# Layer 3's gathered rows as three bfloat16 parts, and fifteen instead of seventeen dense tiles

## The chip, the cores and the metric

The kernel runs on one core of a Trainium2 chip, in one launch. The metric is the device time of that core in microseconds (us), as the median of several runs.

## What is computed

The program is a graph network of four layers on one set of 3750 nodes with 256 features and 60000 edges, sorted by destination. Each layer has a graph part (gnn) and a feed-forward part (ffn). The change concerns layer 3's graph part, two hypergraph convolutions:

```python
def _hconv(x, W, b, src, dst, n):
    xt = x @ W
    ones = jnp.ones(src.shape, xt.dtype)
    D = jax.ops.segment_sum(ones, src, num_segments=n)
    B = jax.ops.segment_sum(ones, dst, num_segments=n)
    Dinv = jnp.where(D > 0, 1.0 / D, 0.0)
    Binv = jnp.where(B > 0, 1.0 / B, 0.0)
    m = jax.ops.segment_sum(xt[src], dst, num_segments=n) * Binv[:, None]
    out = jax.ops.segment_sum(m[dst], src, num_segments=n) * Dinv[:, None]
    return out + b
h = _prelu(_hconv(x, W1, b1, src, dst, n), a)
h = _hconv(h, W2, b2, src, dst, n) + x
return _prelu(h, a)
```

Its input x is the layer norm of the nodes, and its result is added to them. All of it is float32. The destinations are drawn as the square of a uniform number, so low destinations have many edges and high ones few.

## The kernel before, in words

**Tiles.** The nodes are 30 tiles (NT) of 128 (P). Each convolution has three parts: the product with W (`conv_in`, L2245), the sums over edges to the destinations (`to_dst`, L2207), and the sums back to the sources (`to_src`, L2226). Both sums go through `sums` (L2163), in one of two ways.

**Dense.** For the first TD = 17 tiles of destinations there are count matrices: for destination tile t and source tile S a block of 128 x 128 holds the number of edges between each pair of nodes. Tile 0 has so many edges that it has two of them, so there are NV = 18 slabs of 30 blocks. Summing over a block is a matmul. Blocks are bfloat16 (small whole numbers, exact), and the float32 rows are split into three bfloat16 parts whose sum is the row (`split`, L2155: copy, subtract, copy, subtract, on ACT and DVE in turn). So a block costs two matmuls: 512 columns (two parts) into `two_ps` (L2184), and 257 columns (third part and a column of ones that counts the edges) into `third_ps` (L2186).

**Gathered.** The last 13 tiles of destinations have few edges. `CAPS` (L41) gives for every tile the number of chunks of 128 edges: 12 to 10 a tile, 3 for the last, 131 for those 13. For a chunk, POOL issues one indirect DMA (`gather`, L150) that fetches 128 float32 rows of 1 KB from a table in DRAM. DVE compares the place of each edge in its tile with a row of 0 to 127, which makes a one-hot matrix (L2173), and one float32 matmul with 257 columns (L2186) adds the chunk into `third_ps`. Chunks are taken in groups of G = 5 that share a buffer `gt` (five buffers) and a one-hot buffer `oh` (two buffers). ACT puts a column of ones into each `gt` (L2170). Nothing else of these tiles uses `two_ps`.

**To the destinations.** A dense tile loads its slab (`adT`, 960 KB, on SP's queue, four buffers), sums, divides by the count, and is split into `two["m"]`, `third["m"]`, which stay in SBUF. A gathered tile gathers from `xtab`, the table of x @ W, sums, and writes its rows to the table `mtab`. The order is written out: two dense tiles, then thirteen times a gathered and a dense one, then two dense ones.

**To the sources.** For each of the 30 source tiles the same blocks in the other orientation (`ad`, loaded for two source tiles at a time) give 18 dense products with the rows of `m`. The edges to destinations outside the dense tiles are gathered from `mtab`, JS = 5 chunks a source tile. `finish` then makes the tile's result: `between` adds the bias, applies prelu and does the next layer's `conv_in`; `last` (L2259) adds x, updates the nodes and begins the ffn (`enter`).

**conv_in** transposes a tile on PE, multiplies by W, copies the product to SBUF, writes it to `xtab` on SP's queue, and splits it into `two["x"]`, `third["x"]`. The order of instructions on each engine comes from a scheduler that follows the program's priorities; it puts most of the blocks of the first dense tile between the products of the first `conv_in`.

**The blocks** are built during and behind layer 2's ffn by `dense_blocks` (L2068). While edges are read, `put` (L355 to L423) gives each edge a place in a table `blocks` of NCB = 840 columns: NV + SPLIT = 23 columns for each source tile are for dense tiles (the first five slabs have two), JS = 5 for gathered ones. `dense_blocks` reads the first 690 columns, makes one-hots from them (L2112), multiplies pairs of one-hots on PE into one PSUM buffer (L2098), casts on ACT (L2099), transposes them again on PE and writes `adT` and `ad`. There are 36 halves of 15 tiles; some are asked for by layer 2's sums (`beside_l2_sums`, L2064, six at each of its calls), and what is left comes behind the ffn. The other 150 columns are read at the start of `l3_gnn` (L2142), which makes the indices of the gathers from `mtab` from them.

Of the kernel before, what the change touches and what calls it, by code (L numbers as in the profile page):

```python
# [10 lines left out]
F32 = mybir.dt.float32  # L11
# [10 lines left out]
P = 128  # L22
# [11 lines left out]
TD = 17  # L34
NV = TD + 1
SPLIT = 5
JS = 5
# [1779 lines left out]
class Regular(Gnn):  # L1817
# [250 lines left out]
    def dense_blocks(self, pool, wp, op, pp):  # L2068
# [7 lines left out]
        got = pool.tile([P, K], I32, name="db_got")  # L2076
        nc.sync.dma_start(got, self.blocks.rearrange("(p k) a -> p (k a)", p=P)[:, :K])
# [46 lines left out]
    def l3_gnn(self, entry):  # L2124
# [3 lines left out]
        G = 5  # L2128
        with ExitStack() as outer:
            keep, sp, gp, wp, xp, pp, tp, ep = self.pools(outer, l3=1, l3s=4, l3g=5, l3w=2, l3x=2, l3p=-2, l3tp=-1,  # L2130
                                                          l3ep=-2)
# [4 lines left out]

            idx = dict(x=self.srci[:, SP0:], m=keep.tile([P, JS * NT], I32, name="l3_idxm"))
            loc = dict(x=self.dloc[:, SP0:], m=keep.tile([P, JS * NT], F32, name="l3_locm"))
            with ExitStack() as st:
                pool, = self.pools(st, l3i=1)  # L2140
                got = pool.tile([P, JS * NT], I32, name="l3_got")
                nc.scalar.dma_start(got, self.blocks.rearrange("(p k) a -> p (k a)", p=P)[:, NCB - JS * NT:])  # L2142
                part = pool.tile([P, JS * NT], I32, name="l3_part")
                nc.vector.tensor_scalar(part, got, 255, None, op0=ALU.bitwise_and)
                nc.vector.tensor_copy(loc["m"], part)
                nc.vector.tensor_scalar(part, got, 8, None, op0=ALU.arith_shift_right)
                nc.vector.tensor_scalar(idx["m"], part, -float(TD * P), 0.0, op0=ALU.add, op1=ALU.max)

            two, third = {}, {}
            for n, k in (("x", NT), ("m", TD)):  # L2150
                two[n] = keep.tile([P, k, 2, D], BF16, name="l3_two" + n)
                third[n] = keep.tile([P, k, D + 2], BF16, name="l3_third" + n)
                nc.vector.memset(third[n][:, :, D:], 1.0)

            def split(n, t, v):  # L2155
                hm, lo = two[n][:, t], third[n][:, t, :D]
                nc.scalar.copy(hm[:, 0], v)
                r = wp.tile([P, D], F32, name="rest")
                nc.vector.tensor_tensor(r, v, hm[:, 0], ALU.subtract)
                nc.scalar.copy(hm[:, 1], r)  # L2160
                nc.vector.tensor_tensor(lo, r, hm[:, 1], ALU.subtract)

            def sums(n, blocks, table, cols):  # L2163


                rows = []
                for c in range(0, len(cols), G):
                    some = cols[c:c + G]
                    gt = gp.tile([P, G, D + 1], F32, name="gt")
                    nc.scalar.copy(gt[:, :, D], self.ones[:, :G])  # L2170
                    oh = wp.tile([P, G, P], F32, name="oh")
                    k = slice(some[0], some[-1] + 1, some[1] - some[0] if len(some) > 1 else 1)
                    nc.vector.tensor_tensor(oh[:, :len(some)], self.iota.unsqueeze(1).to_broadcast([P, len(some), P]),  # L2173
                                            loc[n][:, k].unsqueeze(2).to_broadcast([P, len(some), P]), ALU.is_equal)
                    for j, k in enumerate(some):
                        self.gather(gt[:, j, :D], table, idx[n][:, k:k + 1])
                        rows.append((oh[:, j, :], gt[:, j, :]))
                ps3 = pp.tile([P, D + 2], F32, name="third_ps")
                all3 = [(block, third[n][:, t, :D + 1]) for block, t in blocks] + rows
                if blocks:  # L2180
                    ps = pp.tile([P, 2, D], F32, name="two_ps")
                for i, (block, rhs) in enumerate(all3):
                    if i < len(blocks):
                        nc.tensor.matmul(flat(ps), block, flat(two[n][:, blocks[i][1]]),  # L2184
                                         start=(i == 0), stop=(i == len(blocks) - 1))
                    nc.tensor.matmul(ps3[:, :D + 1], block, rhs, start=(i == 0), stop=(i == len(all3) - 1))  # L2186
# [6 lines left out]
                if not blocks:  # L2193
                    nc.scalar.mul(o, ps3[:, :D], has)
                    return o
# [6 lines left out]
            def slab_of(v):  # L2202
                slab = sp.tile([P, NV * 2 * P], BF16, name="slab")
                nc.sync.dma_start(slab[:, :NT * P], self.adT[v])
                return slab

            def to_dst(xtab, mtab):  # L2207
                def dense(t):
                    slabs = [slab_of(v) for v in ((0, 1) if t == 0 else (t + 1,))]
                    split("m", t, sums("x", [(slab[:, S * P:(S + 1) * P], S) for slab in slabs for S in range(NT)],  # L2210
                                       None, []))

                def sparse(t):
                    c = sum(CAPS[TD:t])
                    o = sums("x", [], xtab, list(range(c, c + CAPS[t])))
                    nc.sync.dma_start(mtab[(t - TD) * P:(t - TD + 1) * P], o)
                first = TD - (NT - TD) - 2
                for t in range(first):
                    dense(t)
                for i in range(NT - TD):  # L2220
# [90 lines left out]
```

## Time and profile before

| | |
|---|---|
| runs, median (lowest to highest) | 5742.64 us (5733.62 to 5743.11) |
| profiled execution, its own time | 6525.78 us |
| its span; mean granted clock of PE | 6524.0 us; 0.798 |
| busy in it: PE, DVE, POOL, ACT | 70%, 47%, 45%, 32% of the span |
| layer 3's graph part in it | 4749 to 5986 us |
| all matmuls of L2184 and L2186, from blocks and gathers | 2046 and 3284 records |

The profile is one execution in which engines and DMA queues were recorded. Times in windows, waits and chains are us from the start of its span. A row of "waits" names the engine and line that waited, then what it waited for: us in total, times, longest. "issue" is a wait for nothing that the profile shows. In a timeline the bracket is the idle time before an instruction and what ended it. Float32 matmuls leave two records each, and a few records can be missing.

### The profile page before, as it was taken

What the parts mean: (1) busy time and instruction counts of PE and PEld (TensorE: products, weight loads), DVE (VectorE), ACT (ScalarE), POOL (GpSimd) and SP (SyncE); (2) the same over time, 40 slices, a digit from 0 to 9 for tenths busy, and PEclk for the clock granted to TensorE, in tenths of its full rate; (3) what the DMA queues carried; (4) which work ended last, traced back from release to release, by engine and by line L of the source; (5) the groups of instructions that cost most, each with busy time, mean ns of one, the idle gap of its engine ahead of it and who ended that gap; (6) DMA issues with size and microseconds to landing.
All of it is one profiled execution on the core that took longest, in us unless ns stands there. A gap on an engine that the chain in (4) does not pass through costs nothing. (4 is left out here: it accounts for less than half of the span.)

```text
span 6524.0 us, 64749 instructions
## 1 busy us (share of the span) xinstructions
PE 4544.5 (70%) x20324; PEld 3306.5 (51%) x20438; DVE 3068.4 (47%) x7333; ACT 2064.1 (32%) x4862; POOL 2921.8 (45%) x2845
## 2 busy tenths in 40 slices
PE   6826655596476665975555553798879898896885
PEld 2425554465455553634444442576545565564673
DVE  5634433794233346435565557403532342266435
ACT  1125544312455552324343442222531121110121
POOL 0046666676566658864444440012025444452124
PEclk9957777798677777987777775698589999998896
DMA  4334444202344431145555551222434554455113
GB/s 147 132 95 115 115 116 112 43 2 72 99 119 117 115 79 35 22 130 160 159 159 157 147 148 45 90 91 74 162 124 139 137 134 128 132 145 162 50 56 114
DMA packets 431195, 714.02 MB, mean 109 GB/s; under 512 B 117474, under 2 KB 308645, under 8 KB 426748
## 3 DMA queue, kind: packets, MB, share of 16 engines
q0 software_dynamic: 145168, 379.81, 23.0%
q1 hardware_dynamic: 267064, 316.47, 15.5%
q10 hardware_dynamic: 18612, 13.50, 0.7%
q8 instruction: 166, 2.72, 0.2%
q14 instruction: 185, 1.52, 0.1%
HBM read 583.81 MB, written 125.15 MB: 109 GB/s over the span
## 5 line engine op out<-in xcount | busy, mean ns | idle before, releaser
L1965 PE MATMUL sum_ps<-gt,oh 128*128 128x260 f32 (+2 forms) x3150 | 1018.8, 485 | 368.2 <-issue 155.4
L1965 PEld LDWEIGHTS sum_ps<-gt,oh 128*128 128x128 f32 x3150 | 749.4, 244 | 565.0 <-issue 187.7
L150 POOL DMA_INDIRECT gt<-l_vk,srci x525 | 497.6, 948 | 549.1 <-issue 179.4
L156 POOL DMA_INDIRECT blocks<-put x480 | 648.2, 1350 | 155.0 <-issue 145.6
L150 POOL DMA_INDIRECT gt<-l_h,srci x525 | 496.6, 946 | 333.8 <-issue 228.8
L150 POOL DMA_INDIRECT gt<-l_feat,g x525 | 501.7, 956 | 317.2 <-issue 235.2
L1947 DVE TENSOR_TENSOR gt<-gt,bank 128x1792 f32<-128x1792 f32 x225 | 453.5, 2016 | 123.6 <-remote 52.8
L1839 ACT ACTIVATE oh<-iota,dloc 128x128 f32<-128x128 f32 x1575 | 481.4, 386 | 19.1 <-PE sum_ps L1965 15.7
L150 POOL DMA_INDIRECT gt<-l_mtab,l_idxm x300 | 296.3, 988 | 359.9 <-ACT gt L2170 184.3
L150 POOL DMA_INDIRECT gt<-l_xtab,srci x262 | 253.2, 966 | 396.7 <-DMA l_xtab<-xt 192.4
L2184 PE MATMUL two_ps<-l_twox,slab 128*128 128x512 bf16 x1026 | 354.8, 391 | 28.1 <-issue 27.8
L147 PE MATMUL y_ps<-f_w,hT 128*128 128x256 f32 x1600 | 359.4, 384 | 15.5 <-DVE y L1075 13.5
L2184 PEld LDWEIGHTS <-slab 128*128 128x128 bf16 x2160 | 213.5, 99 | 268.2 <-issue 40.9
L2184 PE MATMUL two_ps<-l_twom,slab 128*128 128x512 bf16 x1020 | 341.9, 379 | 0.0
L147 PEld LDWEIGHTS y_ps<-f_w,hT 128*128 128x128 f32 x1600 | 306.8, 193 | 67.2 <-DVE y L1075 18.0
L2186 PE MATMUL third_ps<-l_thirdx,slab 128*128 128x257 bf16 x1080 | 300.7, 280 | 31.5 <-issue 17.6
L2186 PE MATMUL third_ps<-gt,oh 128*128 128x257 f32 x1124 | 275.4, 389 | 37.1 <-DVE oh L2173 28.5
L2186 PE MATMUL third_ps<-l_thirdm,slab 128*128 128x257 bf16 x1080 | 294.8, 273 | 3.2
L1830 ACT ACTIVATE ohT<-rows,iota_p 128x896 f32<-128x896 bf16 x225 | 235.2, 1045 | 142.8 <-DMA rows<-dl_dram 69.7
L1322 PE MATMUL q_ps<-l_qt,ohT 128*128 128x256 f32 x1050 | 250.1, 391 | 31.4 <-DVE gt L1328 18.7
L1976 PE MATMUL bank<-less,at_row 112*128 112x8 f32 (+1 forms) x146 | 41.7, 358 | 317.2 <-issue 156.9
L1922 ACT ACTIVATE fw<-fw 112x128 f32<-112x128 f32 x76 | 23.5, 309 | 754.5 <-DVE fw L1921 608.9
(544 smaller groups left out, 8807.8 us busy)
## 6 DMA issues: line engine op xcount, KB each, us to landing
rows<-dl_dram SPq DMA_DIRECT2D x225, 224.0 KB
slab<-adT SPq DMA_DIRECT2D x36, 960.0 KB
slab<-ad SPq DMA_DIRECT2D x30, 1152.0 KB
l_feat<-ft SPq DMA_DIRECT2D x30, 1040.0 KB
f_w<-in_L_ffn_w_dram SPq DMA_DIRECT2D x18, 1024.0 KB
adT<-db_rowT SPq DMA_DIRECT2D x36, 480.0 KB
ad<-db_row SPq DMA_DIRECT2D x36, 480.0 KB
f_yt<-y SPq DMA_DIRECT2D x114, 128.0 KB
```

The source lines that it names most:

```text
L147: self.nc.tensor.matmul(ps, xT[:, c, :], w[:, c, :], start=(c == 0), stop=(c == kc - 1))
L150: return self.nc.gpsimd.indirect_dma_start(out=out, out_offset=None, in_=table, in_offset=bass.IndirectOffsetOnAxis(ap=idx, axis=0))
L156: inst = self.nc.gpsimd.indirect_dma_start(out=table, out_offset=bass.IndirectOffsetOnAxis(ap=idx, axis=0), in_=src, in_offset=None)
L1322: nc.tensor.matmul(ps[:, j, :], ohT[:, j * P:(j + 1) * P], flat(q[:, ds(tiles[j], 1), :]), start=True, stop=True)
L1830: nc.scalar.activation(t, rows, AF.Abs, bias=self.iota_p, scale=-1.0)
L1839: nc.scalar.activation(oh[:, j, :], self.iota, AF.Abs, bias=self.dloc[:, c + j:c + j + 1], scale=-1.0)
L1922: nc.scalar.activation(fw, fw, AF.Exp)
L1947: nc.vector.tensor_tensor(rows, rows, wj.unsqueeze(3).to_broadcast([P, GC, H, DH]), ALU.mult)
L1965: nc.tensor.matmul(open_[1], oh[:, j, :], gt[:, j, :W], start=starts(k), stop=starts(k + 1))
L1976: nc.tensor.matmul(f_ps, at, less, start=True, stop=True)
L2184: nc.tensor.matmul(flat(ps), block, flat(two[n][:, blocks[i][1]]), start=(i == 0), stop=(i == len(blocks) - 1))
L2186: nc.tensor.matmul(ps3[:, :D + 1], block, rhs, start=(i == 0), stop=(i == len(all3) - 1))
```

## The change

TD goes from 17 to 15, so there are 16 slabs, 15 dense and 15 gathered tiles, 156 chunks in the latter, and JS goes from 5 to 6 (180 instead of 150 gathers a convolution to the sources); `blocks` has 810 columns. Tables `xtab` and `mtab` hold the three bfloat16 parts side by side (768 columns, 1.5 KB a row) and are written after the split. A gathered chunk is then summed like a block: 512 columns into `two_ps` and 257 into `third_ps`, in bfloat16, with a bfloat16 one-hot. Groups are of G = 3 chunks, with eight buffers for rows and for one-hots. Gathered tiles are evicted and split like dense ones. The order is one dense tile, then dense and gathered in turn as long as two dense ones are left, then the gathered ones that are left, and one dense tile. The first `conv_in` has a PSUM pool of its own that is closed before the sums' pools open. The indices of the gathers from `mtab` are made in `dense_blocks`, which reads all columns of `blocks`. There are three slab buffers instead of four.

```diff
@@ -31,10 +31,10 @@
 NB, BP = 5, 112
 GC = 7
 RB = 112
-TD = 17
+TD = 15
 NV = TD + 1
 SPLIT = 5
-JS = 5
+JS = 6
...
@@ -2073,8 +2073,15 @@
         nc = self.nc
         self.adT, self.ad = (self.dram.tile([NV, P, NT * P], BF16, name=n) for n in ("adT", "ad"))
         K = (NV + SPLIT) * NT
-        got = pool.tile([P, K], I32, name="db_got")
-        nc.sync.dma_start(got, self.blocks.rearrange("(p k) a -> p (k a)", p=P)[:, :K])
+        all_got = pool.tile([P, NCB], I32, name="db_got")
+        nc.sync.dma_start(all_got, self.blocks.rearrange("(p k) a -> p (k a)", p=P))
+        got, rest = all_got[:, :K], all_got[:, K:]
+        self.m_idx, self.m_loc = self.kept([P, JS * NT], I32, "m_idx"), self.kept([P, JS * NT], BF16, "m_loc")
+        low = pool.tile([P, JS * NT], I32, name="db_low")
+        nc.vector.tensor_scalar(low, rest, 255, None, op0=ALU.bitwise_and)
+        nc.vector.tensor_copy(self.m_loc, low)
+        nc.vector.tensor_scalar(low, rest, 8, None, op0=ALU.arith_shift_right)
+        nc.vector.tensor_scalar(self.m_idx, low, -float(TD * P), 0.0, op0=ALU.add, op1=ALU.max)
...
@@ -2125,74 +2132,59 @@
         nc, ins = self.nc, self.ins
-        G = 5
+        G = 3
+        R3 = 3 * D
         with ExitStack() as outer:
-            keep, sp, gp, wp, xp, pp, tp, ep = self.pools(outer, l3=1, l3s=4, l3g=5, l3w=2, l3x=2, l3p=-2, l3tp=-1,
-                                                          l3ep=-2)
+            keep, sp, gp, wp, xp = self.pools(outer, l3=1, l3s=3, l3g=8, l3w=2, l3x=2)
...
-            idx = dict(x=self.srci[:, SP0:], m=keep.tile([P, JS * NT], I32, name="l3_idxm"))
-            loc = dict(x=self.dloc[:, SP0:], m=keep.tile([P, JS * NT], F32, name="l3_locm"))
-            with ExitStack() as st:
-                pool, = self.pools(st, l3i=1)
-                got = pool.tile([P, JS * NT], I32, name="l3_got")
-                nc.scalar.dma_start(got, self.blocks.rearrange("(p k) a -> p (k a)", p=P)[:, NCB - JS * NT:])
-                part = pool.tile([P, JS * NT], I32, name="l3_part")
-                nc.vector.tensor_scalar(part, got, 255, None, op0=ALU.bitwise_and)
-                nc.vector.tensor_copy(loc["m"], part)
-                nc.vector.tensor_scalar(part, got, 8, None, op0=ALU.arith_shift_right)
-                nc.vector.tensor_scalar(idx["m"], part, -float(TD * P), 0.0, op0=ALU.add, op1=ALU.max)
-            two, third = {}, {}
+            idx = dict(x=self.srci[:, SP0:], m=self.m_idx)
+            loc = dict(x=keep.tile([P, NS], BF16, name="l3_locx"), m=self.m_loc)
+            nc.vector.tensor_copy(loc["x"], self.dloc[:, SP0:SP0 + NS])
+            iota = keep.tile([P, P], BF16, name="l3_iota")
+            nc.vector.tensor_copy(iota, self.iota)
+            three = {}
             for n, k in (("x", NT), ("m", TD)):
-                two[n] = keep.tile([P, k, 2, D], BF16, name="l3_two" + n)
-                third[n] = keep.tile([P, k, D + 2], BF16, name="l3_third" + n)
-                nc.vector.memset(third[n][:, :, D:], 1.0)
-            def split(n, t, v):
-                hm, lo = two[n][:, t], third[n][:, t, :D]
-                nc.scalar.copy(hm[:, 0], v)
+                three[n] = keep.tile([P, k, R3 + 2], BF16, name="l3_three" + n)
+                nc.vector.memset(three[n][:, :, R3:], 1.0)
+            def split(out, v):
+                nc.scalar.copy(out[:, :D], v)
                 r = wp.tile([P, D], F32, name="rest")
-                nc.vector.tensor_tensor(r, v, hm[:, 0], ALU.subtract)
-                nc.scalar.copy(hm[:, 1], r)
-                nc.vector.tensor_tensor(lo, r, hm[:, 1], ALU.subtract)
-            def sums(n, blocks, table, cols):
-                rows = []
+                nc.vector.tensor_tensor(r, v, out[:, :D], ALU.subtract)
+                nc.scalar.copy(out[:, D:2 * D], r)
+                nc.vector.tensor_tensor(out[:, 2 * D:R3], r, out[:, D:2 * D], ALU.subtract)
+            def sums(n, pp, blocks, table, cols):
+                some3 = [(block, three[n][:, t]) for block, t in blocks]
                 for c in range(0, len(cols), G):
                     some = cols[c:c + G]
-                    gt = gp.tile([P, G, D + 1], F32, name="gt")
-                    nc.scalar.copy(gt[:, :, D], self.ones[:, :G])
-                    oh = wp.tile([P, G, P], F32, name="oh")
+                    gt = gp.tile([P, G, R3 + 2], BF16, name="gt")
+                    nc.scalar.copy(gt[:, :, R3], self.ones[:, :G])
+                    oh = gp.tile([P, G, P], BF16, name="oh")
                     k = slice(some[0], some[-1] + 1, some[1] - some[0] if len(some) > 1 else 1)
-                    nc.vector.tensor_tensor(oh[:, :len(some)], self.iota.unsqueeze(1).to_broadcast([P, len(some), P]),
+                    nc.vector.tensor_tensor(oh[:, :len(some)], iota.unsqueeze(1).to_broadcast([P, len(some), P]),
                                             loc[n][:, k].unsqueeze(2).to_broadcast([P, len(some), P]), ALU.is_equal)
                     for j, k in enumerate(some):
-                        self.gather(gt[:, j, :D], table, idx[n][:, k:k + 1])
-                        rows.append((oh[:, j, :], gt[:, j, :]))
-                ps3 = pp.tile([P, D + 2], F32, name="third_ps")
-                all3 = [(block, third[n][:, t, :D + 1]) for block, t in blocks] + rows
-                if blocks:
-                    ps = pp.tile([P, 2, D], F32, name="two_ps")
-                for i, (block, rhs) in enumerate(all3):
-                    if i < len(blocks):
-                        nc.tensor.matmul(flat(ps), block, flat(two[n][:, blocks[i][1]]),
-                                         start=(i == 0), stop=(i == len(blocks) - 1))
-                    nc.tensor.matmul(ps3[:, :D + 1], block, rhs, start=(i == 0), stop=(i == len(all3) - 1))
+                        self.gather(gt[:, j, :R3], table, idx[n][:, k:k + 1])
+                        some3.append((oh[:, j, :], gt[:, j, :]))
+                ps, ps3 = pp.tile([P, 2, D], F32, name="two_ps"), pp.tile([P, D + 2], F32, name="third_ps")
+                for i, (block, rows) in enumerate(some3):
+                    on = dict(start=(i == 0), stop=(i == len(some3) - 1))
+                    nc.tensor.matmul(flat(ps), block, rows[:, :2 * D], **on)
+                    nc.tensor.matmul(ps3[:, :D + 1], block, rows[:, 2 * D:R3 + 1], **on)
...
                 o = wp.tile([P, D], F32, name="o")
-                if not blocks:
-                    nc.scalar.mul(o, ps3[:, :D], has)
-                    return o
...
             def slab_of(v):
-                slab = sp.tile([P, NV * 2 * P], BF16, name="slab")
+                slab = sp.tile([P, max(NT, 2 * NV) * P], BF16, name="slab")
                 nc.sync.dma_start(slab[:, :NT * P], self.adT[v])
                 return slab
-            def to_dst(xtab, mtab):
+            def to_dst(pp, xtab, mtab):
                 def dense(t):
                     slabs = [slab_of(v) for v in ((0, 1) if t == 0 else (t + 1,))]
-                    split("m", t, sums("x", [(slab[:, S * P:(S + 1) * P], S) for slab in slabs for S in range(NT)],
-                                       None, []))
+                    split(three["m"][:, t], sums("x", pp, [(slab[:, S * P:(S + 1) * P], S)
+                                                           for slab in slabs for S in range(NT)], None, []))
                 def sparse(t):
                     c = sum(CAPS[TD:t])
-                    o = sums("x", [], xtab, list(range(c, c + CAPS[t])))
-                    nc.sync.dma_start(mtab[(t - TD) * P:(t - TD + 1) * P], o)
-                first = TD - (NT - TD) - 2
-                for t in range(first):
+                    row = xp.tile([P, R3], BF16, name="row")
+                    split(row, sums("x", pp, [], xtab, list(range(c, c + CAPS[t]))))
+                    nc.sync.dma_start(mtab[(t - TD) * P:(t - TD + 1) * P], row)
+                tiles, other = list(range(TD)), list(range(TD, NT))
+                dense(tiles.pop(0))
+                while other:
+                    if len(tiles) > 1:
+                        dense(tiles.pop(0))
+                    sparse(other.pop(0))
+                for t in tiles:
                     dense(t)
-                for i in range(NT - TD):
-                    sparse(TD + i)
-                    dense(first + i)
-                for t in range(TD - 2, TD):
-                    dense(t)
-            def to_src(mtab, finish):
+            def to_src(pp, mtab, finish):
                 for S0 in range(0, NT, 2):
-                    slab = sp.tile([P, NV * 2 * P], BF16, name="slab")
-                    rows = slab.rearrange("p (v s) -> p v s", v=NV)
+                    slab = sp.tile([P, max(NT, 2 * NV) * P], BF16, name="slab")
+                    rows = slab[:, :NV * 2 * P].rearrange("p (v s) -> p v s", v=NV)
                     nc.sync.dma_start(rows, self.ad[:, :, S0 * P:(S0 + 2) * P].rearrange("v p s -> p v s"))
                     for i in range(2):
-                        finish(S0 + i, sums("m", [(rows[:, v, i * P:(i + 1) * P], max(v - 1, 0))
-                                                  for v in range(NV)], mtab, list(range(S0 + i, JS * NT, NT))))
+                        finish(S0 + i, sums("m", pp, [(rows[:, v, i * P:(i + 1) * P], max(v - 1, 0))
+                                                      for v in range(NV)], mtab, list(range(S0 + i, JS * NT, NT))))
...
-            xtab, mtab = ([self.dram.tile([k, D], F32, name=f"l3_{n}tab{i}") for i in range(2)]
+            xtab, mtab = ([self.dram.tile([k, R3], BF16, name=f"l3_{n}tab{i}") for i in range(2)]
                           for n, k in (("x", NP), ("m", (NT - TD) * P)))
-            def conv_in(i, t, v):
-                vT = xp.tile([P, 2, P], F32, name="vT")
+            def conv_in(i, t, v, tp):
+                vT = xp.tile([P, 2, P], F32, name="vT", bufs=3)
                 self.transposed(vT, v, tp)
                 ps = tp.tile([P, D], F32, name="xt_ps")
                 self.product(ps, vT, w[i])
-                o = xp.tile([P, D], F32, name="xt")
-                nc.scalar.copy(o, ps)
-                nc.sync.dma_start(xtab[i][t * P:(t + 1) * P], o)
-                split("x", t, o)
-            def between(t, v):
-                nc.vector.tensor_tensor(v, v, bias[0], ALU.add)
-                prelu(v)
-                conv_in(1, t, v)
-            def last(t, v):
+                split(three["x"][:, t], ps)
+                nc.sync.dma_start(xtab[i][t * P:(t + 1) * P], three["x"][:, t, :R3])
+            def last(t, v, ep):
                 nc.vector.tensor_tensor(v, v, bias[1], ALU.add)
-                xn = xp.tile([P, D], F32, name="xn")
+                xn = xp.tile([P, D], F32, name="xn", bufs=3)
                 self.normed(xn, self.x, stats, t)
...
-            for t in range(NT):
-                xn = xp.tile([P, D], F32, name="xn")
-                self.normed(xn, self.x, stats, t)
-                conv_in(0, t, xn)
-            for i, finish in enumerate((between, last)):
-                to_dst(xtab[i], mtab[i])
-                to_src(mtab[i], finish)
+            with ExitStack() as st:
+                tp, = self.pools(st, l3tp=-4)
+                for t in range(NT):
+                    xn = xp.tile([P, D], F32, name="xn", bufs=3)
+                    self.normed(xn, self.x, stats, t)
+                    conv_in(0, t, xn, tp)
+            pp, tp, ep = self.pools(outer, l3p=-2, l3t2=-1, l3ep=-2)
+            def between(t, v):
+                nc.vector.tensor_tensor(v, v, bias[0], ALU.add)
+                prelu(v)
+                conv_in(1, t, v, tp)
+            for i, finish in enumerate((between, lambda t, v: last(t, v, ep))):
+                to_dst(pp, xtab[i], mtab[i])
+                to_src(pp, mtab[i], finish)
...
```

## The prediction

> **What bounds the kernel now.** I read the forty slices first: layer 3's graph convolution is the stretch of slices 29 to 36, where PE is busy eight or nine tenths. Then the windows cut at its stages (us PE, PE load, DVE, ACT and POOL are busy, clock, DMA share, GB/s):
>
> ```profile
> 4510.00:4749.00 239.00, 179.94 (x930) 116.65 (x928) 137.58 (x113) 122.41 (x236) 37.45 (x24) 0.50 0.38 146
> ...
> 4845.00:5080.00 235.00, 203.91 (x1084) 132.73 (x1103) 58.47 (x184) 27.07 (x87) 128.10 (x133) 0.95 0.49 146
> 5080.00:5112.00 32.00, 19.20 (x85) 9.40 (x88) 4.80 (x16) 2.36 (x6) 9.72 (x11) 0.66 0.44 117
> 5112.00:5405.00 293.00, 280.68 (x1535) 185.95 (x1564) 132.07 (x359) 63.68 (x180) 124.53 (x125) 1.00 0.48 129
> ```
>
> 4510 to 4749 builds the dense blocks; 4845 to 5098 sums to the destinations, 5098 to 5405 to the sources; then both come again. Source tiles run at 280.68 of 293 us: PE is the limit. Destination tiles leave PE 31 of 235 us idle, and 12.8 of the 32 us behind them.
>
> The timeline of PE gives the pitch of its matmuls (start, us, operation):
>
> ```profile
> 5112.47 0.38 PE L2184 MATMUL two_ps<-l_twom,slab 128*128 128x512 bf16 x1
> 5112.69 0.27 PE L2186 MATMUL third_ps<-l_thirdm,slab 128*128 128x257 bf16 x1
> 5112.80 2.34 PE L2186 MATMUL third_ps<-gt,oh 128*128 128x257 f32 x10
> 5114.97 0.38 PE L2184 MATMUL two_ps<-l_twom,slab 128*128 128x512 bf16 x1
> ```
>
> Starts count, since durations overlap: 0.22 + 0.11 = 0.325 us for a dense block. Five gathered chunks take ten float32 records from 5112.80 to 5114.97, so 2.17/5 = 0.434 us each.
>
> What stops PE in the destination stage, from the waits of 4845 to 5080 and the timeline of one tile:
>
> ```profile
> PE third_ps L2186 <- DVE oh L2173: 20.1, 6, 11.1
> ```
>
> ```profile
> 4961.72 0.38 PE L2186 MATMUL third_ps<-gt,oh 128*128 128x257 f32 x1 [0.21 <-issue]
> ...
> 4965.25 1.22 PE L2186 MATMUL third_ps<-gt,oh 128*128 128x257 f32 x2 [1.03 <-issue]
> ...
> 4969.90 0.63 PE L2184 MATMUL two_ps<-l_twox,slab 128*128 128x512 bf16 x1
> 4970.54 0.63 PE L2184 MATMUL two_ps<-l_twox,slab 128*128 128x512 bf16 x1
> ```
>
> The first is the one-hots, built into only two buffers. The second I call starvation: with nothing named to wait for, matmuls of gathered rows come 1 to 4 us apart, and afterwards a block takes 0.64 us, at half clock. Each such place begins 12 to 15 us into an unbroken run of gathers on POOL.
>
> **Blocks, 16 slabs instead of 18.** In order of instructions, all four removed halves come out of the tail behind the FFN's last matmul (510 block products there become 450). The chain there alternates between PE and ACT on one PSUM buffer:
>
> ```profile
> 4626.49 0.59 ACT db_rowT L2099
> 4627.09 0.04 issue
> 4627.13 1.11 PE db_psT L2098 x4
> 4628.24 0.02 issue
> 4628.26 0.59 ACT db_rowT L2099
> ```
>
> That is 1.77 us for four tiles, and 6.77 us from half to half (15 tiles). 4 × 6.77 = **-27 us**. The four DVE operations for the gather indices, and 810 instead of 690 columns of places read by SP, move here. They stand ahead of the first one-hot on DVE, at about 0.25 us each by the small DVE rows: 0 to 1 us, I take 0. The same loading leaves layer 3's start, where the conv's own loads hide it: 0.
>
> **To the destinations, twice.** Before, PE has 17 tiles with 18 × 30 dense blocks and 131 gathered chunks: 540 × 0.325 + 131 × 0.434 = 175.5 + 56.9 = 232.4 us. After, 480 blocks and 156 chunks, whose 768 bfloat16 columns need the same 512 and 257 columns as a block: 156.0 + 50.7 = 206.7 us. **-25.7 us a layer, -51 for both.** The measured stages take about 53 us more than their matmuls (first layer: 270 us from the first gather, with 14.6 us of the first dense tile already inside the conv, so 270 - 217.8 = 52; second: 286 - 232 = 54). About 40 of them are starvation and the clock it costs, 14 the one-hots. After: 19% more gathers starve PE in proportion, +8; one-hots get eight buffers, so that their wait could go (-14) or stay (0); I take -7. The destination tiles now alternate dense and gathered up to the last three gathered ones, and only one dense tile follows them instead of two. The first gather from the table of sums came 6 us after the last gathered tile; one dense tile (9.75) and the first source tile's blocks (5.2) give 15 us, where write, 6 gathers and landing need 16 to 17: +1 to +3, I take 3. Net +4 a layer, **+8**.
>
> Gathered tiles gain an eviction of a second bank and the split: ACT 0.372 + 0.404 + 0.405, DVE 0.421 + 0.410 + 0.444 + 0.420 by the rows of the dense tiles. DVE is busy 58 of 235 us and ACT 27, so 15 more of 1.7 and 1.2 us are covered by PE's 9.75 us of the next dense tile. Uncovered they would cost 15 × 2.9 = 43 us a layer; PSUM has two buffers of each, so the next tile need not wait. The write of a gathered tile on SP, now behind the split, is 1.3 us later; it and the slabs queued behind it on SP have three slab buffers (four before), and a slab needs 9.75 us of PE time: 0. But if slabs come late this is the place.
>
> POOL: a gather is 0.946 us and its gap 0.30, so 156 × 1.25 = 195 us, under PE's 207. With a look-ahead of 8 × 3 chunks (5 × 5 before) it starts during the first two dense tiles. Pairs with 12 chunks want 15.0 us of POOL against 13.65 of PE, with 10 chunks 12.5 against 13.0. That is near balance: bounds 0 and 12 us a layer, I take 0 because the head start of 24 gathers (30 us) covers the difference.
>
> **To the sources, twice.** A tile has 18 blocks and 5 chunks before: 5.85 + 2.17 = 8.02 us, and 9.59 to 9.67 measured, the rest being the next conv or the entry. After: 22 × 0.325 = 7.15. -0.87 × 60 = **-52 us**, at full clock. POOL needs 6 × 1.25 = 7.5 of 8.8 us. The conv loses one ACT copy (0.37 us) a tile and its table write waits for the split (1.3 us more); behind that write on SP stands the next slab, three tiles ahead: 0.
>
> **DMA.** A gather goes from 131 to 197 KB. In 5112 to 5405 the queue of gathers took 22.9% of the engines' time and SP's 24.8%. With 1.8 times the bytes, 16/18 of the slabs, and 2 more for the table: 41 + 22 + 2 = 65% of 293 us, 191 of about 266 us, 72%; for the destinations by the same way 77%. The Trainium skill (DMA: Bandwidth & Descriptors, "Anatomy of one DMA") puts only the bytes, at 436 KB per us, on a fixed 2 us: +0.15 us a gather. The trace's packets (4096 bytes in 233 ns, 0.47 us of all 16 engines per gather) give +0.23. I use the trace; by the rule the share would be below 65% and the second rival below smaller.
>
> A rule against the change: "SBUF — State Buffer" (section "SBUF: two separate sides") says that a VectorE operation in a two-port mode locks GpSimd out of writing descriptors. The bfloat16 one-hots are faster operations (the block one-hots do 1920 elements in 1.22 us, the float32 ones 640 in 0.82). If each of about 60 one-hots a stage, at some 0.4 us (scaled from these rows), held POOL up, 24 us a stage would be added, 195 would become 219, and POOL would bound the destinations by 12 us a layer. In the trace a gather takes 942 ns at the least and 946 at the median with DVE at work beside it 45% of the time. I take 0.
>
> **Conv 1** now runs alone in its own PSUM, and the first dense tile follows (19.5 us); before 14.6 us of that lay in the conv's 62. Three matmul groups a tile at 1.55 us are 46 to 50 us: 62 - 48 = 14 won, 14.6 lost: 0 ± 5.
>
> **Sum.** -27 - 51 + 8 - 52 = -122 us. The profiled execution would go from 6525.78 to about 6404 us. It is 13.6% longer than the median of 5742.64, but the stages concerned ran at clocks of 0.94 to 1.00, so I carry the microseconds over, not the share: **5620 us**.
>
> **Rivals.**
> First, more: the new buffers end the one-hot waits and half the starvation goes with them, 46 us more: 5575. For it: 20.1 of the waits are named by one-hots. Against: nothing in the change touches starvation.
> Second, DMA: at 72 to 77% in bursts, the sixth gather lands late, PE waits in each source tile and the -52 is lost: 5672. For it: the shares. Against: landing has four tiles of look-ahead.
> Third, slower: starvation becomes chronic. POOL now has 195 us of gathers in a destination stage of 207, so runs no longer break, which is what started each gap; behind gaps PE goes at 0.64 us a block. If half of 207 us ran so, each layer would lose 103, less the 12 lost now: 2 × 91 - 122 = +60, 5803. It decides from about 61 us more a layer at half clock. Against: PE queues at 0.95 now in that stage, and source tiles with 5 gathers in a row show 1.00.
> The change might also cancel itself, a bit of both: 5735 to 5752.
>
> **Chances.** Forecast 0.50 (5590 to 5650); more 0.20; DMA 0.15; chronic starvation 0.11; no change 0.04. 0.2% is about what a measurement of this kernel tells from no change. Faster 0.85, same 0.04, slower 0.11. The range 5560 to 5700 takes in the first three and leaves out 0.15 and the tails.
>
> **What would show it.** Gathered matmuls as bfloat16 records of 512 and 257 columns at 0.325 us a chunk; source tiles at 8.7 to 8.8 us; the block tail 27 us shorter; one-hot waits under 14 us. It is wrong if source tiles stay at 9.6 with PE waiting on gathers (DMA), or if the clock in the destination stages falls below 0.85 with gaps called issue (starvation).

## The result and the profile after

The changed kernel takes 5650.51 us (median of 4 runs, 5643.41 to 5652.38), the kernel before 5742.51 us (4 runs): ratio 0.9841, 95% interval 0.9824 to 0.9858. That is 92 us faster; 122 were forecast. The profiled execution has a span of 5650.6 us and so fits the runs.

The profile of before shown above does not fit its runs (6525.78 against 5743 us), and that turned out to matter. I therefore profiled the unchanged kernel once more:

> The kernel before, unchanged, profiled once more. Theory A (the record's): the destination stages hold about 53 us of stalls each beyond their matmuls, so they take about 270 and 286 us again, and the source stages 9.6 us a tile. Theory B: those stalls belong to that one profiled execution, which was 783 us longer than the median. Then a profile near 5743 us shows destination stages of about 220 (with part of the first dense tile inside the conv) and 235 us, with no gaps called issue, and the 92 us that the change won are 27 for the blocks, some 45 in the source tiles and 20 for everything else.

It came out at 5747.0 us, span 5745.2 us. Windows of that second profile, one for each stage from the first source stage on: sources, destinations, sources (columns as above):

```profile
4409.00:4698.00 289.00, 277.13 (x1520) 183.32 (x1548) 130.47 (x356) 63.00 (x178) 131.19 (x132) 1.00 0.50 134
4698.00:4935.00 237.00, 235.40 (x1337) 156.98 (x1361) 67.98 (x213) 33.59 (x99) 143.91 (x149) 1.00 0.56 168
4935.00:5219.00 284.00, 263.89 (x1514) 173.93 (x1543) 174.82 (x527) 33.39 (x115) 130.59 (x132) 1.00 0.51 126
```

The destination stage has PE busy for 235.4 of 237 us at full clock. The 53 us of stalls that I read off the first profile are absent from the second, so theory B holds. The same windows of the changed kernel:

```profile
4364.00:4635.00 271.00, 259.64 (x1498) 154.06 (x1496) 135.22 (x388) 54.80 (x180) 172.02 (x179) 0.99 0.73 210
4635.00:4860.00 225.00, 216.32 (x1278) 125.77 (x1276) 94.00 (x301) 42.49 (x149) 156.24 (x159) 0.97 0.71 223
4860.00:5127.00 267.00, 247.37 (x1495) 144.21 (x1493) 177.99 (x556) 39.77 (x143) 171.28 (x178) 1.00 0.67 198
```

All three are shorter, but the destination stage now has 9 us with PE idle and a clock of 0.97. The table cuts both executions by stage (us). A stage ends where DVE takes up the counts of its last tile, right behind that tile's last matmul. (The evictions of `two_ps` would not do: in the kernel before, a source tile's `two_ps` is finished before its five gathered chunks, 2.2 us early.)

| stage | before, second profile | after | difference | forecast |
|---|---|---|---|---|
| up to the last block product | 4107.2 | 4082.5 | -24.7 | -27 |
| first conv and first destinations | 302.3 | 281.6 | -20.7 | -21.7 |
| first sources | 290.6 | 270.6 | -20.0 | -26 |
| second destinations | 234.5 | 225.4 | -9.1 | -21.7 |
| second sources | 286.5 | 266.1 | -20.4 | -26 |
| the rest | 524.1 | 524.4 | +0.3 | 0 |

The forecast for the destinations holds 3 us for the hand-over to the sources; in this cut that hand-over falls into the source stages.

Part of the blocks' difference (2.3 us) had arisen before the first block product. The gathered matmuls came as forecast. In the timeline of PE of the changed kernel a gathered chunk costs what a block does, 0.33 us from start to start:

```profile
4499.67 0.38 PE L2180 MATMUL two_ps<-gt,oh 128*128 128x512 bf16 x1
...
4500.00 0.38 PE L2180 MATMUL two_ps<-gt,oh 128*128 128x512 bf16 x1
...
4500.33 0.38 PE L2180 MATMUL two_ps<-l_threem,slab 128*128 128x512 bf16 x1
...
4501.31 0.38 PE L2180 MATMUL two_ps<-l_threem,slab 128*128 128x512 bf16 x1
```

The three blocks from 4500.33 to 4501.31 took 0.98 us, 0.327 each. Over long stretches the mean is 0.3293 us (155 products in 51.05 us from 4659.82 on), where before it is 0.3258. The end of the second destination stage, on PE, shows what is new:

```profile
4834.47 0.38 PE L2180 MATMUL two_ps<-gt,oh 128*128 128x512 bf16 x1
...
4838.63 0.58 PE L2180 MATMUL two_ps<-gt,oh 128*128 128x512 bf16 x1 [3.67 <-DMA gt<-l_xtab,srci]
...
4843.13 0.59 PE L2180 MATMUL two_ps<-gt,oh 128*128 128x512 bf16 x1 [0.43 <-DMA gt<-l_xtab,srci]
...
4848.17 0.59 PE L2180 MATMUL two_ps<-gt,oh 128*128 128x512 bf16 x1 [0.65 <-DMA gt<-l_xtab,srci]
...
4848.77 0.63 PE L2180 MATMUL two_ps<-l_threex,slab 128*128 128x512 bf16 x1
```

PE waits for gathers, and then its matmuls start 0.64 instead of 0.33 us apart: from 4838.6 to 4851.6 the granted clock is 0.51. The last dense tile, behind the gathers, starts in this stretch. Over the whole stage the waits of PE for gathers are:

```profile
PE two_ps L2180 <- DMA gt<-l_xtab,srci: 8.5, 7, 3.7
```

On POOL, the first and the last gather of that stage:

```profile
4644.68 0.94 POOL L150 DMA_INDIRECT gt<-l_xtab,srci  x1 [38.30 <-PE two_ps L2180]
4645.93 0.94 POOL L150 DMA_INDIRECT gt<-l_xtab,srci  x1 [0.30 <-PE third_ps L2181]
...
4844.47 0.94 POOL L150 DMA_INDIRECT gt<-l_xtab,srci  x1 [0.30 <-issue]
```

156 gathers from 4644.68 to 4845.4 are 1.29 us each, next to the 1.25 of a gather with its gap, so POOL has almost no slack. The first one has to wait until the table `xtab` is complete, whose last write is issued at 4641.9, 2.8 us before. (The bracket names PE, which had long been done; in the first layer the same wait is put down to the write of `xtab`.) Cut along POOL, the stage is 10.1 us until `xtab` is there, 200.7 of gathers, 3.4 to the end of the last gathered matmul, and 11.3 for the last dense tile, 225.5 in all.

### The profile page after: what moved, and what is told of

The parts are those of the page before. It is cut to its first block, busy times and chain, and to the rows that moved or that the text cites. A ratio compares the mean times of both kernels' runs of the same rounds, so it can differ in the third digit from the quotient of the medians.

```text
span 5650.6 us, 64814 instructions
## 1 busy us (share of the span) xinstructions
PE 4363.0 (77%) x20058; PEld 3134.2 (55%) x20058; DVE 3110.9 (55%) x7571; ACT 2056.4 (36%) x4936; POOL 3028.8 (54%) x2955
## 4 chain that ended last, share of the span: by engine, by line
PE 44%; DVE 15%; POOL 12%; issue 9%; DMA 9%; ACT 4%; SPq 0%; DVEq 0%; ACTq 0%; another core or an unknown queue 0%; POOLq 0%
POOL gt L150 11%; PE sum_ps L1965 8%; PE two_ps L2180 7%; PE y_ps L147 5%; PE third_ps L2181 3%; PE hT_ps L1773 3%; PE y_ps L1782 2%; PE h_ps L1566 2%; PE db_psT L2105 2%; PE q_ps L1322 2%; DMA gt<-l_vk,srci 2%; PE qkvs_ps L147 2%; DMA gt<-l_h,srci 2%; PE h_ps L1256 2%; DMA gt<-l_feat,g 2%
## 5 line engine op out<-in xcount | busy, mean ns | idle before, releaser
L150 POOL DMA_INDIRECT gt<-l_xtab,srci x312 | 307.4, 985 | 294.9 <-DMA l_xtab<-l_threex 162.1
L150 POOL DMA_INDIRECT gt<-l_mtab,m_idx x360 | 347.8, 966 | 163.2 <-issue 67.8
L2180 PE MATMUL two_ps<-l_threem,slab 128*128 128x512 bf16 x960 | 322.7, 380 | 0.0
L2180 PE MATMUL two_ps<-l_threex,slab 128*128 128x512 bf16 x960 | 320.0, 382 | 1.3 <-DVE rest L2158 1.3
L2180 PEld LDWEIGHTS <-slab 128*128 128x128 bf16 x1920 | 188.1, 98 | 229.3 <-issue 4.0
L2181 PE MATMUL third_ps<-l_threem,slab 128*128 128x257 bf16 x960 | 262.4, 273 | 0.0
L2181 PE MATMUL third_ps<-l_threex,slab 128*128 128x257 bf16 x960 | 262.2, 275 | 0.0
L2180 PE MATMUL two_ps<-gt,oh 128*128 128x512 bf16 x672 | 233.8, 385 | 18.5 <-DMA gt<-l_xtab,srci 14.5
L1831 ACT ACTIVATE ohT<-ohT,ones 128x896 f32<-128x896 f32 x225 | 234.5, 1042 | 7.3
L1841 ACT ACTIVATE oh<-oh,ones 128x896 f32<-128x896 f32 x225 | 234.4, 1042 | 7.3
```

The costliest lines, as they stand in the source:

```text
L150: return self.nc.gpsimd.indirect_dma_start(out=out, out_offset=None, in_=table, in_offset=bass.IndirectOffsetOnAxis(ap=idx, axis=0))
L1831: nc.scalar.activation(t, t, AF.Relu, bias=self.ones[:, 0:1], scale=-1.0)
L1841: nc.scalar.activation(flat(oh), flat(oh), AF.Relu, bias=self.ones[:, 0:1], scale=-1.0)
L2180: nc.tensor.matmul(flat(ps), block, rows[:, :2 * D], **on)
L2181: nc.tensor.matmul(ps3[:, :D + 1], block, rows[:, 2 * D:R3 + 1], **on)
```

## The experiments

**Each half of the change alone.** `tiles_only` has the kernel before with 15 and 15 tiles in the new order, gathers in float32:

```diff
-TD = 17
+TD = 15
-JS = 5
+JS = 6
...
-                first = TD - (NT - TD) - 2
+                tiles, other = list(range(TD)), list(range(TD, NT))
```

> The kernel before with 15 dense and 15 gathered tiles and six chunks a source tile, in the new order, but with float32 gathers, five chunks a buffer. By matmul counts: blocks -27; destinations 480 x 0.325 + 156 x 0.434 = 223.7 instead of 232.4, -17 for both; sources 16... that is 18 - 2 = 16 blocks and 6 chunks, 7.80 instead of 8.02 us, -13 in all: 5686. Theory C, that the longer gathering needs the narrow rows and the eight buffers: one-hots in two buffers and lone float32 gathered tiles leave PE waiting, and the time is 5715 or more.

Measured: 5679.54 us against 5745.23 on the same chip, ratio 0.9886 (0.9870 to 0.9901), -66. The second destination stage took 225.8 us, -8.7, which is what counting matmuls gives. `parts_only` is the changed kernel with the old tiles:

```diff
-TD = 15
+TD = 17
-JS = 6
+JS = 5
...
-            keep, sp, gp, wp, xp = self.pools(outer, l3=1, l3s=3, l3g=8, l3w=2, l3x=2)
+            keep, sp, gp, wp, xp = self.pools(outer, l3=1, l3s=3, l3g=7, l3w=2, l3x=2)
```

> The changed kernel with 17 dense and 13 gathered tiles and five chunks a source tile as before; bfloat16 parts, groups of three, but seven buffers. By matmul counts: destinations 540 x 0.325 + 131 x 0.325 = 218.1, -29 for both; sources 23 x 0.325 = 7.48 instead of 8.02, -33 in all; first conv up to -9: about 5675. Theory C: if the bfloat16 parts alone are worth less than 40 us, the eviction and split of gathered tiles or the 1.5 times larger gathers take part of it back, 5705 or more.

Measured: 5686.64 us, ratio 0.9899 (0.9884 to 0.9914), -59. The second destination stage took 222.6 us: -11.9, where counting gives -14.3 at 0.325 us a product and -11.4 at the measured 0.3293. In both kernels PE has gaps of less than 2 us there. The windows of that stage, first of `tiles_only`, then of `parts_only`:

```profile
4660.00:4889.00 229.00, 227.34 (x1270) 154.99 (x1293) 68.64 (x211) 33.35 (x102) 156.34 (x162) 1.00 0.57 171
4655.00:4877.00 222.00, 220.40 (x1322) 131.11 (x1345) 89.85 (x293) 41.39 (x141) 143.82 (x149) 1.00 0.71 224
```

So each half alone earns its matmuls there. Together they should give about -20.6; the changed kernel gives -9.1. More than half of that stage's gain is lost only when both are there: its 225.4 us are as long as those of `tiles_only`, which has the same 156 gathers and 14 us more of matmuls. Over the whole program the halves are worth 66 + 59 = 125 us alone and 92 together. Theory C (5715 us or more for the one half, 5705 or more for the other) falls. `parts_only` is still 12 us slower than expected; in its second source stage a tile went from 9.60 to 9.30 us in the mean, -0.30 where counting gives -0.54. Why is open.

**The first conv alone**, in its own PSUM pool with three slab buffers:

```diff
-            keep, sp, gp, wp, xp, pp, tp, ep = self.pools(outer, l3=1, l3s=4, l3g=5, l3w=2, l3x=2, l3p=-2, l3tp=-1,
-                                                          l3ep=-2)
+            keep, sp, gp, wp, xp = self.pools(outer, l3=1, l3s=3, l3g=5, l3w=2, l3x=2)
...
+                tp, = self.pools(st, l3tp=-4)
...
+            pp, tp, ep = self.pools(outer, l3p=-2, l3t2=-1, l3ep=-2)
```

> The kernel before with only the first conv in its own PSUM pool (four buffers) and three buffers for its tiles, three slab buffers as after. The record: neutral, 0 plus or minus 5. From the profile after, where the conv's products take 38 us and the first dense tile 19.5 behind them, against 62 before that included 14.6 of dense work: 47 - 38 = 9 us won at most, 5733 to 5743.

Measured: 5740.71 us, ratio 0.9993 (0.9985 to 1.0001): not told apart from nothing, as forecast (0 ± 5).

**POOL or bytes?** Two kernels take one or the other away. In `fewer_gathers` the number of gathers falls and the matmuls stay; in `two_parts` the gathers stay and lose a third of their bytes:

```diff
-                        self.gather(gt[:, j, :R3], table, idx[n][:, k:k + 1])
-                        some3.append((oh[:, j, :], gt[:, j, :]))
+                        if blocks or j < 2:
+                            self.gather(gt[:, j, :R3], table, idx[n][:, k:k + 1])
+                        some3.append((oh[:, j, :], gt[:, j if blocks else min(j, 1), :]))
```

```diff
-                        self.gather(gt[:, j, :R3], table, idx[n][:, k:k + 1])
+                        self.gather(gt[:, j, :2 * D], table, idx[n][:, k:k + 1])
...
-                    nc.tensor.matmul(ps3[:, :D + 1], block, rows[:, 2 * D:R3 + 1], **on)
+                    nc.tensor.matmul(ps3[:, :D + 1], block, (rows[:, 2 * D:R3 + 1] if i < len(blocks) else rows[:, :D + 1]), **on)
...
```

> The changed kernel, but in the destination stages the third chunk of each group of three is not gathered and its matmul reads the second chunk's rows: 109 gathers instead of 156 a stage, the same matmuls, one-hots and evictions. It leaves out part of the sum over edges. Theory P (POOL, 156 x 1.25 = 195 us behind the table of sums, plus landing and the last dense tile, ends the destination stage of the changed kernel): POOL needs only 136 us, PE's 209 us bound, the second destination stage goes from 225.5 to about 212 us, and the whole is some 25 us under the changed kernel, 5625. Theory D (what costs is the bytes of the gathers on the DMA engines): likewise faster here, so it is told apart by the run with two parts.

> The changed kernel, but gathers fetch only the first two of the three parts (1 KB a row instead of 1.5) and the tables hold only these; the 257 columns of the gathered matmul read the first part again. It leaves out the third part of the gathered rows. Same number of gathers and matmuls. Theory P: POOL's count is the same, so the second destination stage stays at 224 to 226 us and the whole within 8 us of the changed kernel, 5643 to 5651. Theory D (bytes): the destination stages fall to about 212 and source tiles from 8.90 toward 8.75 us; 5615 to 5625.

> The changed kernel with 16 dense and 14 gathered tiles and five chunks a source tile: 143 gathers a destination stage. PE has 510 x 0.329 + 143 x 0.3285 = 214.8 us there. Theory P: POOL ends early enough (179 us), so the stage is bound by PE, 217 to 219 us instead of 225.5 although it has more matmuls; source tiles have 22 products as in the changed kernel, 8.90 us; the blocks cost 12 more: 5645 to 5650. By matmul counts alone the stage would be longer than the changed kernel's, 231, and the whole 5672.

> The changed kernel with five instead of six chunks a source tile (the fullest source tile has 635 edges to gathered destinations, 640 fit): 21 instead of 22 products, 150 instead of 180 gathers in a source stage. By matmul counts 60 x 0.329 = 20 us under the changed kernel, about 5630, destination stages as they were, 225. If source tiles are held by something other than PE's products (the wait of the entry's transposes for DVE, 0.6 us a tile in the second layer), the gain is below 10 us.

These four (with `mid16`, TD = 16 and JS = 5, and `five_chunks`, JS = 5 alone) went to a chip on which the kernel before took 6511.08 us (6494.74 to 6533.06, 15 runs), so none of the expected times can be held against them. They took 6389.76, 6482.98, 6441.42 and 6416.27 us, ratios to before 0.9824, 0.9958, 0.9893 and 0.9854. The second destination stages were 220.5, 274.3, 266.8 and 275.3 us in this order. Even there fewer gathers shorten it by 55 us and fewer bytes by 1 (`five_chunks` has the changed kernel's destination stage). What `mid16` was to show about the balance of POOL and PE stays untested, since all waits are longer there. Three went again, to a chip where before takes 5746.83 us:

> The same kernel as in fewer_gathers (a third chunk of each group in the destination stages not gathered, its matmul reading the second chunk's rows), once more, because in that call the kernel before took 6511 us where it takes 5743 elsewhere. On a chip where before takes 5743: theory P (POOL's 156 gathers end the destination stage) has the second destination stage go from 225.5 to about 212 us and the whole to about 5625. If PE already bounds that stage, it stays above 220.

> The same kernel as in two_parts (gathers fetch two of the three parts; the 257 columns of gathered matmuls read the first part again). On a chip where before takes 5743: theory P has the second destination stage stay at 224 to 226 us and the whole at 5643 to 5651; theory D, that the bytes of the gathers cost, has it fall to about 212, source tiles from 8.90 to 8.75 us, the whole to 5615 to 5625.

> The same kernel as in five_chunks (five chunks a source tile instead of six). On a chip where before takes 5743: by matmul counts 20 us under the changed kernel, 5630, with source tiles at 8.57 instead of 8.90 us; below 10 us if the source tiles are held by something else.

`fewer_gathers_2`: 5626.03 us, ratio 0.9784 (0.9769 to 0.9799). `two_parts_2`: 5646.91 us, 0.9826 (0.9811 to 0.9842), not told apart from the changed kernel. Window of the second destination stage and the waits of PE for gathers in it, of `fewer_gathers_2`:

```profile
4624.00:4836.00 212.00, 210.35 (x1277) 124.36 (x1276) 93.58 (x301) 42.59 (x148) 106.38 (x111) 1.00 0.62 192
```

```profile
PE two_ps L2181 <- DMA gt<-l_xtab,srci: 1.5, 1, 1.5
```

and the window of `two_parts_2`:

```profile
4624.00:4850.00 226.00, 217.53 (x1282) 126.56 (x1280) 94.37 (x303) 42.95 (x151) 157.66 (x161) 0.96 0.58 172
```

With POOL busy 106 instead of 156 us, PE has 1.7 us of gaps and full clock, and the stage is 212.6 us. With the DMA share at 0.58 instead of 0.71 but as many gathers on POOL, it stays at 225.8. Theory P holds: the number of gathers ends the stage, not their bytes.

`five_chunks_2`:

```diff
-JS = 6
+JS = 5
```

5616.01 us, ratio 0.9773 (0.9759 to 0.9786): 34 us under the changed kernel, not 20. A source tile goes from 8.94 to 8.41 us in the first layer and from 8.88 to 8.31 in the second (means of the 29 tiles behind the first), 0.53 and 0.57 for a product of 0.33. It beats both kernels. It fits these edges closely (635 of 640 places in the fullest tile); other edges beyond that take the program's general branch.

**The place of the rows.** `padded` is `five_chunks` with more space between rows:

```diff
-                three[n] = keep.tile([P, k, R3 + 2], BF16, name="l3_three" + n)
+                three[n] = keep.tile([P, k, R3 + 32], BF16, name="l3_three" + n)
...
-                    gt = gp.tile([P, G, R3 + 2], BF16, name="gt")
+                    gt = gp.tile([P, G, R3 + 32], BF16, name="gt")
```

> Five chunks a source tile, and the tiles of three parts and of gathered rows with 800 columns of space for 770 (rows of 1600 instead of 1540 bytes; the same columns are read). In the changed kernel a block takes 0.3293 us from start to start, before 0.3258, where the two parts lay in rows of 1024 bytes. Theory L (the place of the rows in SBUF makes the matmul's reading slower): the pitch goes back to 0.326, 0.0035 x (2 x 636 + 60 x 21) = 9 us less than five_chunks_2, about 5607 where before takes 5743. If it is not the place of the rows, the pitch stays 0.329 and the time within 4 us of 5616.

The pitch, from start to start of the products, is 0.3258 us again, as before the change. Timeline of PE of `padded`:

```profile
4499.89 0.38 PE L2180 MATMUL two_ps<-l_threem,slab 128*128 128x512 bf16 x1
...
4500.21 0.38 PE L2180 MATMUL two_ps<-l_threem,slab 128*128 128x512 bf16 x1
...
4501.84 0.38 PE L2180 MATMUL two_ps<-l_threem,slab 128*128 128x512 bf16 x1
```

(1.95 us for six blocks.) But the time is 5617.22 us, ratio 0.9775 (0.9762 to 0.9789), the same as `five_chunks_2`. Theory L, which expected about 5607, was right about the pitch and wrong about the time: a source tile stays at 8.41 and 8.31 us in the mean, and the second destination stage, with the same 156 gathers, at 224.6 us (226.3 in `five_chunks_2`). The 9 us of matmul time did not shorten the program.

## Why the prediction was right or wrong

**The direction and the main terms were right.** Gathered chunks at the price of blocks, four halves of blocks fewer (-22 within the blocks, -27 forecast), a first conv that does nothing measurable, and the two halves of the change each worth their matmuls in the destination stage.

**The term that was mis-sized is POOL in the destination stage.** I wrote: "That is near balance: bounds 0 and 12 us a layer, I take 0 because the head start of 24 gathers (30 us) covers the difference". The runs give 12.8 us in the second layer (225.4 against 212.6 in `fewer_gathers_2`) and 10.2 in the first (281.6 against 271.4), 23 in both; the whole time differs by 24.5 us (5650.51 against 5626.03, on two chips whose times before differ by 4). The upper end of the bound came close, in part by luck: its working compares pairs of tiles, and the runs show a chain. A head start is used up once: PE did its first two dense tiles before it needed a gather, but POOL could begin only 10 us into the stage, and behind its last gather the landing, that tile's matmuls and a whole dense tile still follow. The comparison should have been 10 + 195 + 15 = 220 us against PE's 207, not 195 against 207. (That sum is made after the fact, with the changed kernel's own figures; the other 5 us are waits between POOL's gathers.) With the measured term, -122 + 23 = -99, and -92 was measured; the rest is smaller errors of both signs.

The first destination stage, at -20.7 for -21.7, looks as forecast in part by luck: it lost 10.2 us to POOL as well, and in the profile of `conv_only` that stage is 4 us shorter than in the second profile of before (298.4 against 302.3), which I had not taken.

**The stalls I carried over were not there.** I took 53 us of stalls a layer from the first profile and let them stay, +8 net for both layers. In the second profile the stage is 2 us longer than its matmuls (234.5 against 232.4). Since I took the stalls on both sides, the error in the sum is only 2 us; the other 6 of the +8 are the hand-over, which came. I had noted that this execution was 13.6% longer than the median and used the microseconds all the same, because the clock looked whole.

**Source tiles: right in kind, 6 us a layer too much.** Forecast -26 a layer, measured -20.0 and -20.4. One part is the hand-over, +3 a layer in my sum, which lies in these stages: the first source tile took 11.5 us in the first layer and 8.5 in the second, where its 22 products are 7.2: 4 and 1 us for the hand-over. In the first layer PE waits 3.0 us there for gathers from `mtab`, and then goes at half clock. The other 29 tiles fell from 9.74 to 8.94 us and from 9.60 to 8.88 (means), -0.80 and -0.72, not -0.87. With the measured pitches the products alone fall by 0.79 (18 × 0.3258 + 5 × 0.434 before, 22 × 0.3293 after). That the pitch is the cause is still not shown, since `padded` takes it away and leaves a tile as long as in `five_chunks_2`.

These tiles do not follow PE's products alone. In the second layer PE also idles for DVE before the entry's transposes. The waits of the kernel before (27 tiles), of the changed one (24) and of `five_chunks_2` (23):

```profile
PE en_ps L1385 <- DVE en_xn L133: 17.1, 27, 0.6
PE en_ps L1385 <- DVE en_xn L133: 15.8, 24, 0.7
PE en_ps L1385 <- DVE en_xn L133: 11.0, 23, 0.7
```

That is 0.63, 0.66 and 0.48 us a tile. The wait was there before, so it is not what the change lost. But where a tile gained more than its products, it is shorter: in `five_chunks_2`, and in `tiles_only`, where it is 0.24 us and the tile fell by 0.65 for 0.22 us of products. Which instruction order makes the difference was not tried.

**The rivals.** More, 5575: one-hots and starvation could not vanish, as they were not there. DMA: the shares came near the estimates (0.73 and 0.67 in the source stages for 72%, 0.71 in the second destinations for 77%), but `two_parts_2` shows that the bytes cost nothing measurable in the destination stage. Chronic starvation: the clock of the destination stage stayed at 0.97; the rival's point of 61 us at half clock a layer was not reached. POOL without a break did cost, but by its own length at the end of the stage. The rule on locked descriptors: bfloat16 one-hots took 0.55 us each, more than the 0.4 I had scaled, and in the changed kernel a gather still takes 946 ns at the median (940 at the least). The 156 gathers took 200.7 us with all their waits, 6 more than 195, where the rule would have added 24; no lock shows.

## What to carry to other kernels

When the work of an engine that feeds another comes close to the other's (here 195 us against 207), add its chain from end to end: when it may start, its length, and what must follow its last piece. A head start does not shorten that chain. Two changes that each pay alone can meet on the next bound, so test the halves as well as the whole; and before stalls are costed from a profile, see that its time is that of the runs.

## What was not expected of the hardware

The same program took about 5745 us on some chips and 6511 us on another, and the profiled execution shown at first (6525.78 us) looks like the latter. Whether it is the chip or the hour is not separated. With the same matmuls and the same 949 ns gathers, the second destination stage of `five_chunks` there had these waits of PE and its weight load (5316 to 5591 us):

```profile
PEld L2180 <- issue: 34.4, 59, 2.0
...
PEld L2181 <- DVE o L2190: 18.1, 10, 4.2
...
PE two_ps L2180 <- DVE o L2189: 14.0, 10, 4.8
...
PE third_ps L2181 <- issue: 13.4, 16, 2.2
```

With a third fewer gathers (`fewer_gathers`) the stage took 220.5 instead of 275.3 us there, so most of this goes with the number of gathers, as it does not with their bytes (274.3 in `two_parts`). What PE lacks when it waits for "issue" is not shown by these profiles and stays open, and so does what the changed kernel itself takes on that chip.

A matmul of bfloat16 rows that lie 1540 bytes apart took about 1% longer than one of rows 1600 bytes apart (a block 0.3293 against 0.3258 us). Whether the distance itself or the place where a row starts does it was not tried.
